# A graph attention layer: more edges get their keys and values by one-hot matmuls, and ScalarE writes a bias

## The chip, the cores and the metric

The kernel runs on one core of a Trainium2 chip. A core has TensorE (PE; matmuls, which write PSUM), VectorE (DVE), ScalarE (ACT), GpSimd (POOL) and SyncE (SP); each takes its instructions in order, and they wait for one another by semaphores. PEld is TensorE's weight load, which lies beside its matmuls. DMAs are issued from SP's and ACT's queues with addresses known to the queue, or from POOL's, which here reads 128 row numbers from SBUF and gathers those rows ("indirect DMA"). The metric is the device time of one execution in microseconds.

## What is computed

A graph has 6250 nodes with 64 features and 206250 edges sorted by destination. The reference, cut to what matters:

```python
Qh = (x @ Wq.T + bq).reshape(n, H, D)          # n = 6250, H = 4 heads, D = 16
Kh = (x @ Wk.T + bk).reshape(n, H, D)
Vh = (x @ Wv.T + bv).reshape(n, H, D)
Ee = (edge_attr @ We.T + be).reshape(-1, H, D)
score = (Kh[src] * Qh[dst] * (1.0 / np.sqrt(D)) * Ee).sum(-1)
score = jnp.exp(jnp.clip(score, -5.0, 5.0))
msg = Vh[src] * score[..., None]
wV = jax.ops.segment_sum(msg, dst, num_segments=n)
x = _layernorm(x + wV.reshape(n, H * D), axis=-1)
```

## The kernel before

**Tiles and steps.** 128 edges are a tile (1612 of them), 8 tiles a group. A step is two groups (16 tiles), the last eight steps one group each: 105 steps (`STEPS`, `NS`). The loop over steps starts at L708. In it the program text gives every engine its order by hand (`manual_schedule`); there is no planner.

**Before the loop.** k and v of all nodes are made and written to a table in DRAM (`kv_tab`, L315 to L324), then q in three bf16 parts (L340 to L361). The first four groups get k and v from gathered rows of x instead of the table (L230, L368 to L384): two transposes, an ACT copy, a bias matmul, two f32 matmuls and an ACT copy for each half group. Steps 2 and 3 are gathered (L402) before the branch at L412, whose other side handles unsorted inputs and does not run here.

**A step.** For step s: `products` (L602, L603: k times q times edge value, DVE), `scores` (L609 to L612: sum over a head, clip, exponent on ACT), `message` (L619 on DVE, L622 on ACT: v times score, and its first bf16 part), `minus` twice (L630, L632: the second and third bf16 part by a matmul with minus the identity), and in the next step `sums` (L638: 16 matmuls with the one-hot of destinations) and `add` (L652). For step s+1 it makes the one-hot rows (`spread` L555 on TensorE, L572 and L577 on ACT), the edge values (`edges`, L388 for the bias and L391), and the queries (L595). `small` (a PSUM tile) holds scores, sums and the row numbers that picking needs.

**k and v of a step** lie in one of five buffers `kvs`. They come in three ways. (1) Gathers on POOL: `gather(s+4)` stands behind `message(s)`, and its buffer is set free by that very product, so POOL starts when L619 is through. (2) Picking, for steps 4 to 94 (`picks_in`, L67), fills the last two tiles of step s+2: `sources` (L466, ACT) and `sources_turned` (L471, TensorE) spread the source numbers along the partitions; `hots` (L481, DVE, four for a step: two tiles, two halves) compares them with 25 block numbers at a time; `picks` (L491) multiplies 50 one-hot blocks with the table `parts` (x in three bf16 parts, 128 rows by 50 blocks), 25 matmuls a call; `picked` (L498, DVE) adds the three parts; `picked_turned` and `picked_kv` (L505 to L516) make k and v with f32 matmuls. Each picked tile is one gather less. (3) In every sixth step one column is fetched row by row from SP's queue (`fetch_rows`, L528 to L544; 16 or 24 rows in a step), which is one gather less in that step.

**The table `parts`** is set to zero (L427) behind the branch and made in steps 0 to 3 from seven loads of x (L448), with three ACT copies (L450, L451, L457) and two DVE subtractions (L456, L458) for each load.

The order of a step in the code, as the change finds it, starts with `onehot_rows` of the first next group and `sums(s-1)`, then `sources_turned`, `products(s)`, `edges(s+1, 0)`, `picks(s, 0, 0)`, `scores`, `onehot_rows_rest` of the second group, `message`, `gather`, `edges(s+1, 1)`, `minus`, `picks(s, 0, 1)`, `minus`, `picked_kv(s-1)`, `picks(s, 1, 0)`, `queries(s+1)`, `picks(s, 1, 1)`, and the hots of the next step. Sources for step s+1 and s+2 are prepared a step ahead.

## Time and profile before

| what | us |
|---|---|
| median of 10 runs (3072.1 to 3083.85) | 3078.01 |
| the profiled execution | 3074.86 |
| its span, first to last instruction | 3072.8 |
| busy: PE, PEld, DVE, ACT, POOL | 1982, 1554, 1504, 918, 1341 |
| mean granted TensorE clock (share of full) | 0.785 |
| gathers on POOL (L402), 1383 | 1308.5 |
| pick matmuls (L491), 9100 | 1040.7 |
| one-hots for picking (L481), 364 | 651.5 |

"Busy" is the time in which an engine has an instruction under way; matmuls overlap, so a matmul's mean duration is longer than the distance between two. "Idle before" a group is the time for which the engine stood still ahead of it, with what ended the wait; "issue" there means that the profile shows nothing it waited for, and "remote" that the releaser could not be named. In a timeline the columns are start, busy time, engine, line, operation, output<-inputs, shape and count, and in brackets the idle time before. In a table by stretches of time a row has the stretch, its length, busy time and number of instructions for PE, PEld, DVE, ACT and POOL, then the granted clock, the DMA share and GB/s.

### The profile page before, as it was taken

How to read it: one execution, taken by the hardware profiler on the slowest of the kernel's cores; microseconds unless marked ns; L12 is line 12 of the kernel's file. 1: busy time of each engine (PE TensorE's matmuls, PEld its weight loads, DVE VectorE, ACT ScalarE, POOL GpSimd, SP SyncE). 2: the span in 40 equal slices, each digit the busy share in tenths (PEclk: the TensorE clock that was granted, in tenths of full speed). 3: DMA queues.
4: the chain of work that ended last, by engine and by line, in shares of the span. 5: the costliest groups of instructions: out<-in, count | busy, mean ns of one | idle time of the engine just before them, and what ended most of it. 6: DMA issues, size and time to landing. Idle time of an engine off the chain costs nothing. (4 is left out here: it accounts for less than half of the span.)

```text
span 3072.8 us, 44286 instructions
## 1 busy us (share of the span) xinstructions
PE 1982.3 (65%) x15751; PEld 1554.2 (51%) x15751; DVE 1503.8 (49%) x1695; ACT 918.3 (30%) x1328; POOL 1340.6 (44%) x1427
## 2 busy tenths in 40 slices
PE   4546666657666666657566666757576666667665
PEld 4334555545454554545454554545454555545553
DVE  3234545545454545545454544545454554445554
ACT  2242332323232323323232232323232232223334
POOL 5455435344444434343444435343444434353342
PEclk9967878778787877778787877777787877777885
DMA  5222112111111111111111111111211111111111
GB/s 149 66 77 60 54 45 58 49 51 51 48 46 53 55 44 54 53 58 44 56 53 46 55 43 58 43 56 43 60 48 54 48 51 56 43 58 42 51 57 32
DMA packets 109970, 166.71 MB, mean 54 GB/s; under 512 B 69196, under 2 KB 71452, under 8 KB 109626
## 3 DMA queue, kind: packets, MB, share of 16 engines
q0 software_dynamic: 45280, 91.78, 10.4%
q1 hardware_dynamic: 64074, 71.01, 7.8%
q8 instruction: 125, 2.05, 0.3%
q10 hardware_dynamic: 384, 1.00, 0.2%
q14 instruction: 107, 0.88, 0.1%
HBM read 156.33 MB, written 7.33 MB: 53 GB/s over the span
## 5 line engine op out<-in xcount | busy, mean ns | idle before, releaser
L402 POOL DMA_INDIRECT kv<-kv_tab,src_i x1383 | 1308.5, 946 | 1677.0 <-DVE pq L619 1237.6
L491 PE MATMUL pick<-parts,hot 128*128 128x192 bf16 x9100 | 1040.7, 275 | 251.3 <-issue 250.6
L491 PEld LDWEIGHTS <-hot 128*128 128x128 bf16 x9100 | 890.3, 109 | 380.4 <-issue 323.3
L481 DVE TENSOR_TENSOR hot<-small,block 128x3200 bf16<-128x3200 bf16 x364 | 651.5, 1818 | 274.8 <-remote 247.9
L595 PE MATMUL pq<-qw,to 126*128 126x64 bf16 x1612 | 167.1, 220 | 679.7 <-issue 583.7
L572 ACT ACTIVATE to<-pb,minus_row 126x1024 bf16<-126x1024 f32 x202 | 223.0, 1104 | 1012.3 <-PE pb L555 958.1
L602 DVE TENSOR_TENSOR prod<-kv,pq 128x1024 f32<-128x1024 f32 (+2 forms) x105 | 123.7, 1178 | 799.4 <-PE pq L595 408.8
L595 PEld LDWEIGHTS <-to 126*128 126x128 bf16 x1612 | 109.3, 112 | 753.0 <-issue 750.3
L632 ACT ACTIVATE msg<-pq 128x1024 bf16<-128x1024 f32 (+2 forms) x210 | 207.8, 990 | 743.4 <-remote 480.2
L391 PE MATMUL pe<-we_sb,et 128*128 128x128 f32 x1612 | 247.9, 300 | 0.0
L391 PEld LDWEIGHTS pe<-we_sb,et 128*128 128x128 f32 x1612 | 207.9, 202 | 55.5 <-issue 50.6
L577 ACT ACTIVATE to<-to,one_p 126x1024 bf16<-126x1024 bf16 x202 | 230.4, 1141 | 3.5
L609 DVE TENSOR_REDUCE small<-prod 128x64 f32<-128x1024 f32 (+2 forms) x105 | 124.4, 1185 | 191.7 <-PE small L471 147.2
L638 PEld LDWEIGHTS <-of 128*128 128x128 bf16 x1612 | 156.6, 108 | 48.6 <-issue 37.7
L638 PE MATMUL small<-msg,of 128*128 128x192 bf16 x1612 | 171.6, 265 | 0.5 <-ACT msg L632 0.5
L630 PE MATMUL pq<-msg,minus_b 128*128 128x512 bf16 x404 | 126.9, 393 | 61.2 <-ACT msg L622 47.6
L555 PE MATMUL pb<-key_rows,ident_b 112*128 112x512 bf16 x403 | 151.4, 464 | 5.9 <-issue 4.7
L622 ACT ACTIVATE msg<-pq 128x1024 bf16<-128x1024 f32 (+2 forms) x105 | 103.9, 990 | 96.0 <-DVE pq L619 96.0
L603 DVE TENSOR_TENSOR prod<-prod,pe 128x1024 f32<-128x1024 f32 (+2 forms) x105 | 123.6, 1177 | 3.6
L619 DVE TENSOR_TENSOR pq<-kv,small 128x1024 f32<-128x1024 f32 (+2 forms) x105 | 123.5, 1176 | 1.4 <-ACT small L612 1.4
L585 DVE TENSOR_TENSOR of<-small,key 128x2048 bf16<-128x2048 bf16 (+2 forms) x105 | 123.2, 1173 | 0.3
L498 DVE TENSOR_REDUCE xp<-pick 128x128 f32<-128x384 f32 x91 | 50.8, 558 | 101.5 <-PE pick L491 101.5
(129 smaller groups left out, 991.3 us busy)
## 6 DMA issues: line engine op xcount, KB each, us to landing
et<-in_eT SPq DMA_DIRECT2D x100, 512.0 KB
rk<-kv_tab SPq DMA_DIRECT2D x1920, 0.5 KB
kv<-kv_tab,src_i POOLq DMA_INDIRECT x1383
qw<-q_tab SPq DMA_DIRECT2D x202, 15.8 KB
kv_tab<-kv_sb SPq DMA_DIRECT2D x5, 640.0 KB
q_tab<-q SPq DMA_DIRECT2D x5, 480.0 KB
acc<-in_x SPq DMA_DIRECT2D x48, 32.0 KB
out<-y SPq DMA_DIRECT2D x48, 32.0 KB
```

Source lines behind the costliest of these rows:

```text
L391: nc.tensor.matmul(pe[:, 2 * u:2 * u + 2, :], et[:, u, :], we_sb, start=False, stop=u == n // 2 - 1, skip_group_check=True)
L402: nc.gpsimd.indirect_dma_start(out=kv_of(g)[:, j, :], out_offset=None, in_=kv_tab[:, :], in_offset=bass.IndirectOffsetOnAxis(ap=src_i[:, t ...
L481: nc.vector.tensor_tensor(HOT[s, i, h].rearrange("p b (a c) -> p b a c", c=2), pairs(from_b[i])[:, None].to_broadcast(shape), block2[:, bl ...
L491: nc.tensor.matmul(rows3[:, i], hot[:, k, :], parts[:, b], start=b == 0, stop=b == NB - 1)
L555: nc.tensor.matmul(pb[:, b:b + 4, :], ident_b[:NR2, g // 2:g // 2 + 1].to_broadcast([NR2, P]), key_rows[:, g % 2, b * P:(b + 4) * P], star ...
L572: nc.scalar.activation(TO[g][:, :n, :], pb[:3 * W, :n, :], AF.Square, bias=minus_row3[:3 * W])
L577: nc.scalar.activation(TO[g][:, :n, :], TO[g][:, :n, :], AF.Relu, bias=one_p[:3 * W], scale=-1.0)
L595: nc.tensor.matmul(PQ[s][:, (g - STEPS[s][0]) * G + j, :], TO[g][:, j, :], QW[g], start=j == 0, stop=j == tiles_of(g) - 1, skip_group_chec ...
L609: nc.vector.tensor_reduce(score, prod[:, :n, :].rearrange("p g (h d) -> p g h d", h=H), axis=AX.X, op=OP.add)
L630: nc.tensor.matmul(msg[:, lo:hi, :], minus_b, M3[s][:, lo:hi, i, :], start=False, stop=True, skip_group_check=True)
L632: nc.scalar.activation(M3[s][:, :n, i + 1, :], msg[:, :n, :], AF.Copy)
L638: nc.tensor.matmul(PA[s], OH[s][:, j, :], M3[s][:, j], start=j == 0, stop=j == n - 1)
```

## The change

Picking starts at step 0 and ends two steps later (steps 0 to 96). In steps 0, 4, 8, ... 92 a third tile of step s+2 is picked, in the PSUM room of the second one: its half picks stand ahead of the queries, `picked_third` adds them up, and both halves of the second tile follow the queries. Step 2 and 3's picked tiles are not gathered before the branch. The table `parts` is made before the branch from the transposed x that is there anyway: 13 blocks of up to four transposes, two ACT copies and two DVE subtractions each, between the halves of the first k and v, which now turn the next half's x ahead of the current half. From step 1 on the edge values' bias is written into their PSUM tile by an ACT copy of a broadcast (`biases`), behind the exponent, and the bias matmul L388 is left out in the loop. `edges(s+1, 0)` moves behind `picked_turned`, `onehot_rows_rest` of the second group behind both edges. The column fetched row by row is the one before (index 12), as 13 can be picked now. The one-hots have six buffers instead of four, `far` three. Three buffers of the branch that does not run are made smaller.

```diff
 XG = 4
-TB = 8
-M0 = 4
+THIRD = 4
...
-LAST = NS - 8 - 3
+LAST = NS - 8 - 1
 def picks_in(s):
-    return M0 <= s <= LAST
+    return 0 <= s <= LAST
+def picks_third(s):
+    return picks_in(s) and s % THIRD == 0 and STEPS[s + 2][1] == 2
+def is_picked(g, j):
+    s = max(s for s in range(NS) if STEPS[s][0] <= g)
+    return picks_in(s - 2) and g == groups_of(s)[-1] and j >= (G - 3 if picks_third(s - 2) else G - 2)
...
-COLUMN = 2 * G - 3
+COLUMN = 2 * G - 4
...
+    parts = consts.tile([P, NB, 3, C], BF16, name="parts")
+    be_all = consts.tile([P, C], F32, name="be_all")
...
+        nc.sync.dma_start(be_all, beT.to_broadcast([P, C]))
...
+        halves = []
+        def parts_of_x(b):
+            n = min(TB, NB - b)
+            px = npsum.tile([P, 2, 2 * C], F32, name="ps").rearrange("p i (j c) -> p (i j) c", j=2)
+            px = px[:, :n]
+            for u in range(n):
+                nc.tensor.transpose(px[:, u, :], xT_sb[:C, (b + u) * P:(b + u + 1) * P],
+                                    ident[:C, :C])
+            nc.scalar.activation(parts[:, b:b + n, 0], px, AF.Copy)
+            nc.vector.tensor_sub(px, px, parts[:, b:b + n, 0])
+            halves.append((px, b, n))
+        def rest_of_x():
+            px, b, n = halves.pop(0)
+            nc.scalar.activation(parts[:, b:b + n, 1], px, AF.Copy)
+            nc.vector.tensor_sub(parts[:, b:b + n, 2], px, parts[:, b:b + n, 1])
+        order = [(g, h) for g in range(XG) for h in range(2)]
+        blocks = list(range(0, NB, TB))
+        xe = x_turned(*order[0])
+        for i, gh in enumerate(order):
+            following = x_turned(*order[i + 1]) if i + 1 < len(order) else None
+            for b in blocks[2 * i:2 * i + 2]:
+                parts_of_x(b)
+            first_kv(*gh, xe)
+            xe = following
+            while halves:
+                rest_of_x()
+    def edge_values(pe, et, n, biased=False):
+        if not biased:
+            nc.tensor.matmul(pe[:, :n, :], ones_b, be_p[:, :n, :], start=True, stop=False,
+                             skip_group_check=True)
...
     for g in range(XG, 2 * KVB - 2):
         for j in range(G):
-            gather_kv(g, j)
+            if not is_picked(g, j):
+                gather_kv(g, j)
...
-            parts = accp.tile([P, NB, 3, C], BF16, name="parts")
-            nc.vector.memset(parts, 0.0)
-            NX = N // NB
...
+            pe_all = fixed.tile([P, 2 * G, C], F32, name="pe")
...
-            def table_parts(b):
-                n = min(TB, NB - b)
-                raw = work.tile([P, TB, C], F32, name="raw", bufs=1)
-                nc.sync.dma_start(raw[:NX, :n], x_v[:, b:b + n, :])
-                rest = pick[:NX, :n * C].rearrange("p (b c) -> p b c", b=n)
-                nc.scalar.activation(rest, raw[:NX, :n], AF.Copy)
-                nc.scalar.activation(parts[:NX, b:b + n, 0], raw[:NX, :n], AF.Copy)
...
+            def wanted(s, i):
+                return picks_third(s) if i == 2 else picks_in(s)
...
-                if picks_in(s):
-                    FAR[s, i] = work.tile([P, P], BF16, name="far")
-                    nc.scalar.activation(FAR[s, i], row50, AF.Identity,
-                                         bias=src_f[:, s - M0, i:i + 1], scale=-1.0)
+                if wanted(s, i):
+                    FAR[s, i] = work.tile([P, P], BF16, name="far", bufs=3)
+                    nc.scalar.activation(FAR[s, i], row50, AF.Identity, scale=-1.0,
+                                         bias=src_f3[:, thirds.index(s):][:, :1] if i == 2 else
+                                         src_f[:, s, i:i + 1])
...
-                if picks_in(s):
-                    HOT[s, i, h] = work.tile([P, NB // 2, P], BF16, name="hot", bufs=4)
+                if wanted(s, i):
+                    HOT[s, i, h] = work.tile([P, NB // 2, P], BF16, name="hot", bufs=6)
...
-                if picks_in(s):
+                if wanted(s, i):
                     hot = HOT.pop((s, i, h))
                     for k in range(NB // 2):
                         b = h * NB // 2 + k
-                        nc.tensor.matmul(rows3[:, i], hot[:, k, :], parts[:, b], start=b == 0,
-                                         stop=b == NB - 1)
+                        nc.tensor.matmul(rows3[:, min(i, 1)], hot[:, k, :], parts[:, b],
+                                         start=b == 0, stop=b == NB - 1)
+            def picked_third(s):
+                if picks_third(s):
+                    X[s] = work.tile([P, 3, C], F32, name="xp")
+                    nc.vector.tensor_reduce(X[s][:, 0], rows3[:, 1].rearrange("p i c -> p c i"),
+                                            axis=AX.X, op=OP.add)
...
                 if picks_in(s):
                     room = psum.tile([P, G, P], F32, name="pb")
-                    nc.tensor.transpose(room[:, 0, :], X[s].rearrange("p k c -> p (k c)"), ident)
-                    xe = work.tile([P, P], F32, name="xe")
-                    nc.scalar.activation(xe, room[:, 0, :], AF.Copy)
-                    X[s] = xe, room[:, 4:6, :]
+                    xe = work.tile([P, 2, P], F32, name="xe")
+                    nc.tensor.transpose(room[:, 0, :], X[s][:, 1:].rearrange("p k c -> p (k c)"), ident)
+                    if picks_third(s):
+                        nc.tensor.transpose(room[:C, 1, :], X[s][:, 0], ident)
+                    nc.scalar.activation(xe[:, 0], room[:, 0, :], AF.Copy)
+                    if picks_third(s):
+                        nc.scalar.activation(xe[:C, 1], room[:C, 1, :], AF.Copy)
+                    X[s] = xe, room[:, 4:7, :]
             def picked_kv(s):
                 if picks_in(s):
                     xe, kv = X.pop(s)
-                    nc.tensor.matmul(kv, ones_b, bkv_p[:, :2], start=True, stop=False,
+                    lo = 0 if picks_third(s) else 1
+                    n = tiles_in(s + 2)
+                    nc.tensor.matmul(kv[:, lo:], ones_b, bkv_p[:, lo:3], start=True, stop=False,
                                      skip_group_check=True)
-                    nc.tensor.matmul(kv, xe, wkv, start=False, stop=True, skip_group_check=True)
-                    nc.scalar.activation(kvs[(s + 2) % KVB][:, 2 * G - 2:, :], kv, AF.Copy)
+                    nc.tensor.matmul(kv[:, 1:], xe[:, 0], wkv, start=False, stop=lo == 1,
+                                     skip_group_check=True)
+                    if lo == 0:
+                        nc.tensor.matmul(kv[:, 0], xe[:C, 1], wkv[:C, 0], start=False, stop=True,
+                                         skip_group_check=True)
+                    nc.scalar.activation(kvs[(s + 2) % KVB][:, n - 3 + lo:n, :], kv[:, lo:], AF.Copy)
...
-                        if not picks_in(s - 2) or g == STEPS[s][0] or j < G - 2:
+                        if not is_picked(g, j):
                             gather_kv(g, j)
...
             def edges(s, k):
                 g = STEPS[s][0] + k
-                if k == 0:
-                    PE[s] = psum.tile([P, 2 * G, C], F32, name="pe")
-                edge_values(PE[s][:, k * G:(k + 1) * G], ET[g], tiles_of(g))
+                PE[s] = pe_all
+                edge_values(PE[s][:, k * G:(k + 1) * G], ET[g], tiles_of(g), s > 0)
+            def biases(s):
+                n = tiles_in(s)
+                nc.scalar.activation(pe_all[:, :n, :], be_all[:, None, :].to_broadcast([P, n, C]),
+                                     AF.Copy)
...
             closed, scaled, normed = 0, 0, 0
+            for i in (0, 2):
+                sources(0, i)
+                sources_turned(0, i)
...
+            sources(0, 1)
+            sources(1, 0)
+            for i, h in ((0, 0), (0, 1), (2, 0)):
+                hots(0, i, h)
...
                     sums(s - 1)
                 sources_turned(s, 1)
                 sources_turned(s + 1, 0)
+                sources_turned(s + 1, 2)
...
-                making = [b for b in range(s * 2 * TB, (s + 1) * 2 * TB, TB) if b < NB]
-                if making:
-                    rest = table_parts(making[0])
                 prod = products(s)
                 picked(s - 1)
-                if more:
-                    edges(s + 1, 0)
                 picks(s, 0, 0)
                 score = scores(s, prod)
-                if nexts[1:]:
-                    onehot_rows_rest(nexts[1])
+                if more:
+                    biases(s + 1)
                 if s:
                     add(s - 1)
                 msg = message(s, score)
                 if s + KVB - 1 < NS:
                     gather(s + KVB - 1)
                 picked_turned(s - 1)
+                if more:
+                    edges(s + 1, 0)
                 if nexts[1:]:
                     edges(s + 1, 1)
+                    onehot_rows_rest(nexts[1])
                 minus(s, msg, 0)
                 hots(s, 1, 0)
+                hots(s, 2, 1)
                 picks(s, 0, 1)
+                picks(s, 2, 0)
                 minus(s, msg, 1)
+                picks(s, 2, 1)
                 picked_kv(s - 1)
                 if not more:
                     close(B - 2)
                     spreads(B - 2)
                 hots(s, 1, 1)
-                picks(s, 1, 0)
+                if not picks_third(s):
+                    picks(s, 1, 0)
                 sources(s + 1, 1)
                 sources(s + 2, 0)
+                sources(s + 2, 2)
                 if s + 1 < NS:
                     rows_fetched(s + 1)
                 if more:
...
                         keys(nexts[0] * G)
                     onehot_edges(s + 1)
                     queries(s + 1)
-                picks(s, 1, 1)
+                if not picks_third(s):
+                    picks(s, 1, 1)
                 hots(s + 1, 0, 0)
+                picked_third(s)
+                if picks_third(s):
+                    picks(s, 1, 0)
+                    picks(s, 1, 1)
                 hots(s + 1, 0, 1)
+                hots(s + 1, 2, 0)
                 if more:
                     while closed < B - 2 and due[closed] <= s:
...
                         if normed < scaled:
                             norm(normed)
                             normed += 1
-                for i, b in enumerate(making):
-                    if i:
-                        rest = table_parts(b)
-                    table_parts_rest(b, rest)
             assert normed == B - 2
```

Line numbers of before are those of the profile.

## The prediction

> **What bounds the kernel now.** I read the page first, then the times at which the message product (DVE, L619) starts, which cut the run into steps, then TensorE inside one step, then clock and gathers beside it.
>
> The page (share of the span; then groups: busy, mean ns | idle before, releaser):
>
> ```profile
> span 3072.8 us, 44286 instructions
> PE 1982.3 (65%) x15751; PEld 1554.2 (51%) x15751; DVE 1503.8 (49%) x1695; ACT 918.3 (30%) x1328; POOL 1340.6 (44%) x1427
> ...
> L402 POOL DMA_INDIRECT kv<-kv_tab,src_i x1383 | 1308.5, 946 | 1677.0 <-DVE pq L619 1237.6
> L491 PE MATMUL pick<-parts,hot 128*128 128x192 bf16 x9100 | 1040.7, 275 | 251.3 <-issue 250.6
> ...
> L595 PE MATMUL pq<-qw,to 126*128 126x64 bf16 x1612 | 167.1, 220 | 679.7 <-issue 583.7
> ```
>
> No engine is full. The gathers wait for the messages, not the reverse, and TensorE stands idle 680 us before its query matmuls, 584 of it for nothing that the profile shows. TensorE in step 39 (message at 1301.87), in order of time:
>
> ```profile
> 1304.41 0.59 PE L630 MATMUL pq<-msg,minus_b 128*128 128x512 bf16 x2
> 1304.84 2.23 PE L491 MATMUL pick<-parts,hot 128*128 128x192 bf16 x25
> ...
> 1308.17 1.79 PE L491 MATMUL pick<-parts,hot 128*128 128x192 bf16 x18
> ...
> 1314.42 0.37 PE L595 MATMUL pq<-qw,to 126*128 126x64 bf16 x4 [2.16 <-issue]
> ...
> 1323.11 0.53 PE L595 MATMUL pq<-qw,to 126*128 126x64 bf16 x7 [1.18 <-issue]
> 1323.45 4.19 PE L491 MATMUL pick<-parts,hot 128*128 128x192 bf16 x25
> 1327.43 0.74 PE L555 MATMUL pb<-key_rows,ident_b 112*128 112x512 bf16 x2
> 1328.01 1.49 PE L638 MATMUL small<-msg,of 128*128 128x192 bf16 x16
> ```
>
> Up to 1309.5 it runs without a gap, then it starts some 17 matmuls in 13.6 us, 0.7 or 1.4 us apart, and at 1323.1 it runs freely again. The 14 gathers of the step (POOL) start from 1303.35 to 1319.61. I call the time from 1309.5 to 1323.1 the slow stretch. It ends 2.6 us after the last gather in every step that I looked at, so it belongs to the gathers. The 25 picks behind it take 4.19 us, those ahead of it 2.23, as the granted clock says (sixth figure after the stretch's length):
>
> ```profile
> 1302.00:1314.00 12.00, 8.88 (x80) 6.91 (x79) 8.10 (x6) 3.11 (x5) 8.21 (x9) 1.00 0.16 45
> 1314.00:1327.60 13.60, 5.93 (x42) 4.93 (x42) 4.01 (x4) 1.33 (x4) 5.03 (x6) 0.50 0.25 73
> ```
>
> So a step is: gathers, slow stretch (over 21.3 us after the message), then what TensorE has left, picks first, then sums and the score that ends in the next message: 9.3 us. Message products of selected steps:
>
> ```profile
> 204.70 1.22 DVE L619 TENSOR_TENSOR pq<-kv,small 128x1024 f32<-128x1024 f32 x1
> 228.13 1.22 DVE L619 TENSOR_TENSOR pq<-kv,small 128x1024 f32<-128x1024 f32 x1
> ...
> 2294.78 1.22 DVE L619 TENSOR_TENSOR pq<-kv,small 128x1024 f32<-128x1024 f32 x1
> 2325.43 1.22 DVE L619 TENSOR_TENSOR pq<-kv,small 128x1024 f32<-128x1024 f32 x1
> 2353.05 1.22 DVE L619 TENSOR_TENSOR pq<-kv,small 128x1024 f32<-128x1024 f32 x1
> ...
> 2964.51 1.22 DVE L619 TENSOR_TENSOR pq<-kv,small 128x1024 f32<-128x1024 f32 x1
> 2979.93 1.22 DVE L619 TENSOR_TENSOR pq<-kv,small 128x1024 f32<-128x1024 f32 x1
> ```
>
> Step 72: 30.65 us with picks and 14 gathers. Step 73: 27.62 with picks and 13 gathers. Step 2: 23.43 with no picks and 14 gathers. Step 95: 15.42 with no picks and 8 gathers, where step 92 (message at 2895.40, next 2919.27) takes 23.87 with picks and 8. A pick is not free: its matmuls sit where TensorE is on the path, and a gather taken away gives back less.
>
> The sum is made against the profiled execution, 3074.86 us (2.06 around its span). The median of the runs is 3.15 above it.
>
> **The change part by part.**
>
> *Picks in steps 0 to 3.* The old intervals from message 0 (153.46) to message 4 (251.77) sum to 98.3. With picks they become like step 4 (picks, 14 gathers, no row fetches yet on SP): 251.77 to 281.26, 29.5. One of the four is a third-pick step (29.5 + 4, below), one has 13 gathers (27.7), two have 14: 120. **+22**, ends +14 (all 28) and +34 (all like step 72). The loads and copies of the old table (7 loads on SP, 21 ACT copies of 0.55, 14 DVE subtractions of 0.64) leave these steps; they lay in the slow stretch, where DVE waited 7 to 11 us, so I count nothing for them.
>
> *Before the loop.* Steps 2 and 3 gather 27 tiles, not 32. Gathers start 1.25 apart (72.38, 73.63), and the making of q crawls until 109, behind the last of them: -6. The first k and v (L375 to L384) run 3.03 us per half, eight halves, TensorE without a gap (114.92 to 139.5). The change puts 50 transposes of 64 rows in between. Nearest row is L350 (64 columns, f32): 12 in 2.79, so 0.23 each, +11.5 (ends 0, and 16 by L375's 0.32). The 26 ACT copies (0.38 by L378) and 26 DVE subtractions lie beside it. Ahead of message 0 the 4.06 us memset of the table goes and three hots of 1.82 come; DVE waited 1.23 there, so about +1. One more load of the edge bias on SP is early and hidden. **+6.5**, ends 0 and +13.
>
> *The third pick.* 24 steps (0, 4, ... 92); 22 of them between step 4 and 91. Each adds 50 picks on TensorE, two hots (3.6 us) and one reduce on DVE, one ACT copy of 0.39 and one of 0.27, one transpose and one or two small matmuls. DVE's and ACT's share is covered: DVE waits 8.16 us ahead of L602 in step 39, ACT 9.73 ahead of L572. Where that cover went, 4.2 us of DVE would come on the path. TensorE has no such cover. Ahead of the slow stretch it is busy without a gap, in the stretch it gets through its 17 whatever they are, so 50 more go behind it. The order puts the queries ahead of both halves of pick 1, so the products start no later, but sums(s) still follow the last pick. Price: behind the stretch the first 25 or so run at 0.16, as before; by then 4.6 us have passed and the clock is 1.00 (1327.6 on), so 50 at 0.083 (2.23 for 25, less the overlap) are 4.1, and 0.1 for the small ones. 4.2 x 22 = **+92**. Ends: 2.1 each if half of them are covered (+46); 8.3 if all run at half clock (+183). I take the full clock, since the rows at 1327.43 on show it. In pick 1 a wait is added: its first matmul needs the DVE reduce of the third pick. Queued behind it are 50 picks and the sums. The three key and value matmuls and 16 queries stand between (some 1.5 us), which hides a 0.56 reduce.
>
> The Trainium skill, page "TensorE: Matmul & The Clock Gate", section "What's actually happening", says that about 3.4 us of sustained work give the full clock. By that rule the stretch at half clock would be 1.2 us shorter than the 4.6 seen, and the added picks still run warm: the same 92.
>
> *Fewer gathers.* 22 intervals lose one gather. Step 76 (14 gathers, 16 row fetches on SP, 2414.32 to 2444.22) takes 29.90, step 73 with as many row fetches and 13 gathers 27.62: -2.3 here, about -2.1 over all such steps; the end of the slow stretch itself moves by 1.45 (21.3 to 19.85). Step 73 has its TensorE order unchanged, the new steps carry more, so I take -1.8: **-40**, ends -28 (1.25, a gather's own spacing) and -62 (2.8, step 72 to 73).
>
> The same skill, page "SBUF — State Buffer", section "Who interferes with whom", says that DMA never contends with a compute engine. By it a gather less would shorten nothing and this term would be 0; the trace (13.6 us of crawl beside 14 gathers, less beside 13) speaks against it.
>
> *The bias.* Two matmuls of L388 go per step (0.31 between starts, 0.62 in all), and an ACT copy of 128x1024 comes (1.02 by L622). It stands where L577 (1.14) stood, between the exponent and the first message copy, and L577 moves behind the latter; there ACT idled 0.88 before L622 and 7.3 before the second L632. So ACT pays nothing; if it came on the path, the first L632 starts 0.4 later, +20 with half the steps. TensorE's 0.62 lies ahead of L630, which starts at 1304.41, while L622 ends at 1304.15: only 0.15 to 0.2 can be won. What is late next is that ACT copy. 92 x -0.15 = **-14**, ends -57 and +20. The edge values of the first group move behind the first picks and are needed a step later: nothing.
>
> *The end.* Steps 95 and 96 get picks: 15.42 to 23.9 (step 92), 14.41 to about 22.4. Step 94 gets its last 25: 21.31 to 23.9. Step 92 is a third (+4), and 92 and 93 each lose two gathers of 1.22. Sum **+18**, ends +10 and +24. The steps behind are half as large and their gathers start as before.
>
> Sum: 22 + 6.5 + 92 - 40 - 14 + 18 = +84.5, so 3159 on the profiled execution and some 3162 on the median; I say 3160.
>
> **The rivals.**
> A (forecast): the third pick lies bare behind the slow stretch. 3160; its own range 3115 to 3215.
> B (faster): the extra picks go where TensorE idles, because the stretch limits something other than the number of matmuls. For it: 584 us of idle with no releaser. Against it: steps 5 to 92 alike get through 6 to 23 matmuls there, picks or queries. Third pick 0 gives 84.5 - 92 = -7.5, 3067; with the bias at its end 3024. It decides where a third pick costs under 0.36 us.
> C: TensorE stays at half clock through all picks: 4.1 more, 22 times: 3250. For it: the slow stretch is when the clock falls. Against: 1.00 is granted 4.6 us after it.
> D: ACT's new copy delays the message chain by 0.4 to 1 us: 37 to 92 more, 3197 to 3252. Against: the 0.88 of idle.
>
> **How the numbers follow.** A 0.62, B 0.10, C 0.12, D 0.12; 0.04 for no change within 0.2%, which is about what a measurement of this kernel can tell. All low ends together give 3026, all high 3321; leaving 2 in 10 out gives 3076 to 3250. Faster 0.10, same 0.04, slower 0.86.
>
> **What would show it.** Right: intervals of steps 4, 8, 12 near 34 to 35 us with 75 to 85 matmuls behind the slow stretch before L638, its end unmoved; intervals 5, 9, 13 near 28.5; the others within 0.5 of before; steps 0 to 3 near 30. The bias right: L630 0.1 to 0.2 sooner after the message. Wrong: if the third-pick steps are as long as their neighbours, the picks found cover; if all steps shorten by half a microsecond or more, the bias was on the path; if steps 0 to 3 stay near 24, picks are cheaper than they look.

## The result and the profile after

The changed kernel takes 3158.36 us in the median of 8 runs (3155.53 to 3167.25), the kernel before 3078.24 in 28 runs beside it: ratio 1.0266, 95% interval 1.0257 to 1.0275. The change makes the kernel slower, by 80 us, where 82 were forecast (3160 against 3078). The profiled execution of after took 3165.68 us, 7.3 above its median; that of before lies 3.2 below its own. So the traces differ by 90.8 us, and the shares below are shares of that.

The page of after: engines, then the groups that answer to those shown of before (gathers, picks, queries).

```profile
span 3163.9 us, 48270 instructions
PE 2107.1 (67%) x17533; PEld 1685.1 (53%) x17533; DVE 1631.1 (52%) x1811; ACT 1013.0 (32%) x1509; POOL 1303.0 (41%) x1391
...
L449 POOL DMA_INDIRECT kv<-kv_tab,src_i x1347 | 1271.0, 944 | 1802.0 <-DVE pq L681 1363.7
L531 PE MATMUL pick<-parts,hot 128*128 128x192 bf16 x10900 | 1227.0, 270 | 382.4 <-issue 379.5
...
L657 PE MATMUL pq<-qw,to 126*128 126x64 bf16 x1612 | 155.3, 223 | 514.5 <-issue 433.2
```

36 gathers fewer free 37.5 us of POOL, which waits for messages anyway (its idle time ahead of the gathers went from 1677 to 1802). 1800 picks more are 186 us of TensorE's busy time. Its idle time ahead of the queries shrank by 165 us and that ahead of the picks grew by 131: in the steps with a third pick, the slow stretch is now filled with picks, where queries stood in it.

Message products of a step with a third pick (40), of the one behind it with 13 gathers (41), and the first steps:

```profile
157.70 1.23 DVE L681 TENSOR_TENSOR pq<-kv,small 128x1024 f32<-128x1024 f32 x1 [0.28 <-ACT small L674]
191.55 1.22 DVE L681 TENSOR_TENSOR pq<-kv,small 128x1024 f32<-128x1024 f32 x1
219.60 1.22 DVE L681 TENSOR_TENSOR pq<-kv,small 128x1024 f32<-128x1024 f32 x1
...
1384.49 1.22 DVE L681 TENSOR_TENSOR pq<-kv,small 128x1024 f32<-128x1024 f32 x1
1418.05 1.22 DVE L681 TENSOR_TENSOR pq<-kv,small 128x1024 f32<-128x1024 f32 x1
1446.61 1.22 DVE L681 TENSOR_TENSOR pq<-kv,small 128x1024 f32<-128x1024 f32 x1
```

The gathers that run after message s are those for step s+5, since message s frees the buffer of that step (there are five); in the program text they stand behind message s+1. So step 41 has 13 gathers because of the third pick of step 44, which fills a tile of step 46.

Step 40 takes 33.56 us, step 41 28.56. Over the 22 steps of each kind between 4 and 91, the mean interval went from 30.30 to 34.22 where a third pick is made, from 29.92 to 28.43 in the step behind it, from 30.40 to 30.39 and from 29.55 to 29.69 in the other two. Interval 0 (with a third pick) is 33.85, interval 1 28.05; they were 26.71 and 24.53.

TensorE in step 40, in order of time (start, length, and in brackets the idle time before):

```profile
1387.24 4.29 PE L531 MATMUL pick<-parts,hot 128*128 128x192 bf16 x50
1391.37 0.59 PE L692 MATMUL pq<-msg,minus_b 128*128 128x512 bf16 x2
...
1396.70 0.41 PE L531 MATMUL pick<-parts,hot 128*128 128x192 bf16 x3 [1.69 <-issue]
1398.10 0.32 PE L531 MATMUL pick<-parts,hot 128*128 128x192 bf16 x1 [0.99 <-issue]
...
1407.02 1.01 PE L657 MATMUL pq<-qw,to 126*128 126x64 bf16 x16
1407.84 5.64 PE L531 MATMUL pick<-parts,hot 128*128 128x192 bf16 x50
1413.31 0.60 PE L612 MATMUL pb<-key_rows,ident_b 112*128 112x512 bf16 x2
1413.75 1.49 PE L700 MATMUL small<-msg,of 128*128 128x192 bf16 x16
```

The picture is that of before with 50 picks more in it. TensorE runs freely to 1392, crawls until about 1406.3, which is 21.8 us after the message (21.3 before), and then has all 50 picks of the second tile in front of the sums, where before it had 25. (I call the slow stretch the crawl as well.) The table of stretches of step 40 (as before: matmuls in brackets, granted clock in the sixth figure after the length):

```profile
1384.49:1396.50 12.01, 8.84 (x84) 7.54 (x85) 9.27 (x7) 3.36 (x5) 8.09 (x9) 1.00 0.15 44
1396.50:1406.30 9.80, 3.43 (x14) 1.56 (x14) 0.12 (x1) 0.36 (x1) 5.13 (x6) 0.52 0.15 43
1406.30:1418.00 11.70, 11.58 (x117) 10.18 (x115) 8.02 (x13) 5.61 (x9) 0.00 (x0) 0.81 0.19 52
```

117 matmuls stand behind the crawl up to the next message, TensorE is busy for 11.58 of the 11.70 us, and POOL has nothing to do there.

Step 40 is one of the mildest. In the mean of the 20 steps with a third pick from 12 to 91, the crawl (taken up to the last idle time of TensorE over 0.3 us ahead of the sums) ends 21.55 us after the message, where it ended at 21.30 in the same steps of before. From there to the sums TensorE does 76 matmuls (68 to 85) in 8.32 us, where it did 30 in 4.69; what follows the sums is as long as before (4.30 against 4.34). So the whole 3.9 us lies between the crawl and the sums.

### The profile page after: what moved, and what is told of

It reads as the page before. It is cut to its first block, busy times and chain, and to the rows that moved or that the text cites. A ratio compares the mean times of both kernels' runs of the same rounds, so it can differ in the third digit from the quotient of the medians.

```text
span 3163.9 us, 48270 instructions
## 1 busy us (share of the span) xinstructions
PE 2107.1 (67%) x17533; PEld 1685.1 (53%) x17533; DVE 1631.1 (52%) x1811; ACT 1013.0 (32%) x1509; POOL 1303.0 (41%) x1391
## 5 line engine op out<-in xcount | busy, mean ns | idle before, releaser
L449 POOL DMA_INDIRECT kv<-kv_tab,src_i x1347 | 1271.0, 944 | 1802.0 <-DVE pq L681 1363.7
L531 PE MATMUL pick<-parts,hot 128*128 128x192 bf16 x10900 | 1227.0, 270 | 382.4 <-issue 379.5
L531 PEld LDWEIGHTS <-hot 128*128 128x128 bf16 x10900 | 1032.5, 107 | 562.5 <-issue 481.6
L521 DVE TENSOR_TENSOR hot<-small,block 128x3200 bf16<-128x3200 bf16 x436 | 773.4, 1816 | 0.0
L657 PE MATMUL pq<-qw,to 126*128 126x64 bf16 x1612 | 155.3, 223 | 514.5 <-issue 433.2
L438 PE MATMUL pe<-we_sb,et 128*128 128x128 f32 x1612 | 215.0, 287 | 48.7 <-ACT pe L626 46.4
L438 PEld LDWEIGHTS pe<-we_sb,et 128*128 128x128 f32 x1612 | 194.0, 196 | 73.9 <-ACT pe L626 70.4
L538 DVE TENSOR_REDUCE xp<-pick 128x64 f32<-128x192 f32 x24 | 8.6, 358 | 305.9 <-PE pick L531 232.5
L612 PE MATMUL pb<-key_rows,ident_b 112*128 112x512 bf16 x403 | 140.2, 433 | 1.0 <-ACT to L634 1.0
```

What stands on the lines that cost most here:

```text
L438: nc.tensor.matmul(pe[:, 2 * u:2 * u + 2, :], et[:, u, :], we_sb, start=False, stop=u == n // 2 - 1, skip_group_check=True)
L449: nc.gpsimd.indirect_dma_start(out=kv_of(g)[:, j, :], out_offset=None, in_=kv_tab[:, :], in_offset=bass.IndirectOffsetOnAxis(ap=src_i[:, t ...
L521: nc.vector.tensor_tensor(HOT[s, i, h].rearrange("p b (a c) -> p b a c", c=2), pairs(from_b[i])[:, None].to_broadcast(shape), block2[:, bl ...
L531: nc.tensor.matmul(rows3[:, min(i, 1)], hot[:, k, :], parts[:, b], start=b == 0, stop=b == NB - 1)
L612: nc.tensor.matmul(pb[:, b:b + 4, :], ident_b[:NR2, g // 2:g // 2 + 1].to_broadcast([NR2, P]), key_rows[:, g % 2, b * P:(b + 4) * P], star ...
L657: nc.tensor.matmul(PQ[s][:, (g - STEPS[s][0]) * G + j, :], TO[g][:, j, :], QW[g], start=j == 0, stop=j == tiles_of(g) - 1, skip_group_chec ...
```

## The experiments

Each kernel was compared with the kernel before on the same chip, and four chips were used. Before took 3073.99 us on the chip of a1_no_third, a2_bias_matmul, a3_third_no_matmuls and b1_no_picks, 3095.02 on that of b2_no_picks_no_rows, b3_half_gathers, c1_early_pick and c2_late_pick, 3081.36 on that of b4_no_rows, c3_pick_last and c5_pick_last_no_rows, and 1790.08 on that of c6_late_pick_no_rows, which is a finding of its own, told there. Totals are compared across chips only as ratios to before.

**Undoing parts of the change.** Three kernels start from after.

*a1_no_third* makes no third pick; everything else of the change stays.

```diff
 def picks_third(s):
-    return picks_in(s) and s % THIRD == 0 and STEPS[s + 2][1] == 2
+    return False
```

> The changed kernel without the third pick: the tile is gathered again, all else is as changed. Theory T (matmuls behind the slow stretch lie bare): the third-pick intervals fall from 34.2 to 30.3 us (24 times, -93) and the intervals that had one gather less get 1.45 us longer (23 times, +34), net -59 from 3158: 3100. Rival M (the cost lies in the moved order, the bias copy or the early and late picks): it stays above 3140.

Measured: 3094.47 us, ratio 1.0075 (1.0057 to 1.0092). The four kinds of steps have means of 30.26, 29.59, 30.27 and 29.58, as before the change (30.30, 29.92, 30.40, 29.55). The third pick is 1.9 of the 2.7 per cent; the picks of steps 0 to 3 and the rest are 0.75.

*a2_bias_matmul* gives the bias of the edge values back to TensorE.

```diff
-                edge_values(PE[s][:, k * G:(k + 1) * G], ET[g], tiles_of(g), s > 0)
+                edge_values(PE[s][:, k * G:(k + 1) * G], ET[g], tiles_of(g))
...
-                if more:
-                    biases(s + 1)
```

> The changed kernel with the bias matmul back in place of the ScalarE copy, order as changed. Theory T by the two traces, in which the intervals of plain steps stayed at 30.4 us: 3153 to 3163. Rival W (the copy wins 0.15 us a step, as the prediction had it): 3172. Rival X (the copy is itself in the way, TensorE waited 46 us for it in the changed kernel): 3110 to 3145.

Measured: 3156.86 us, ratio 1.0282 (1.0261 to 1.0303), against 1.0266 (1.0257 to 1.0275) with the copy on ScalarE: no difference that can be told. The run changes both at once, so it shows that the exchange is worth nothing, not what each side is. The traces add where the gain went: with the copy, the first matmul of `minus` starts 2.33 us after the message in the median step (2.54 in before, 2.55 to 2.66 in a2_bias_matmul), so TensorE is 0.2 us sooner there, and the steps without a third pick are no shorter for it (30.39 and 29.69 against 30.32 and 29.63).

*a3_third_no_matmuls* keeps the third pick's one-hots, reduce, transposition and copies, and the gather it saves, but does 2 of its 50 matmuls, so the third tile's k and v are not computed.

```diff
                     for k in range(NB // 2):
+                        if i == 2 and k != h * (NB // 2 - 1):
+                            continue
                         b = h * NB // 2 + k
```

> The changed kernel with 2 of the 50 matmuls of each third pick, so that the third tile's keys and values are wrong; its one-hots, its reduce, its copies and its gather left out are as changed. Theory T (TensorE pays): the third-pick intervals fall by 3.9 us and the shorter gathers stay, 3158 - 93 = 3065. Rival V (DVE's two one-hots and the wait on the reduce pay): above 3140.

Measured: 3073.32 us, ratio 0.9999 (0.9989 to 1.0009). Steps with a third pick fall from 34.22 to 30.65, the steps behind stay at 28.25. So 48 matmuls are 3.57 us of a step, 0.074 each, and the two one-hots of 1.8, the reduce, the copies and the 2 matmuls left are together no more than about 0.4 (30.65 against 30.26 in a1_no_third, on the same chip). In this kernel the gathers saved make up for all the rest of the change.

**What picks cost at all.** *b1_no_picks* is the kernel before with no pick: all 16 tiles of a step gathered.

```diff
 def picks_in(s):
-    return M0 <= s <= LAST
+    return False
...
-            nc.vector.memset(parts, 0.0)
...
-                making = [b for b in range(s * 2 * TB, (s + 1) * 2 * TB, TB) if b < NB]
+                making = []
```

> The kernel before with no picks at all: 16 gathers in every step (15 where a column is fetched row by row), no one-hots, no table. Theory T: the slow stretch ends 1.49 + 16 x 1.22 + 2.4 = 23.4 us after the message and 2.6 us of work follow as in step 3 of before, so 26 us instead of 30.0 in steps 4 to 91: about 2700. Rival P (a pick earns its place: two gathers more cost 2.1 to 2.8 us each): 3300 or more.

Measured: 2745.78 us, ratio 0.8921 (0.8899 to 0.8944). It is faster than both kernels. Without picks the intervals from 4 to 91 have a mean of 26.59 us, with two picks and two gathers fewer 30.04. What follows the last gather is short here: from its start to the next message product 6.4 us in the mean of steps 12 to 89, against 12.5 in the kernel before and 13.5 in after. The sums start 8.2 us after the message here, ahead of the last gather's end in every step from 12 to 89; in before they start at 25.7 and in after at 26.4, behind it in every step. TensorE has nothing left by then (step with messages at 1294.13 and 1319.43, one with 15 gathers; granted clock in the sixth figure after the length):

```profile
1302.00:1312.00 10.00, 7.08 (x38) 4.89 (x36) 2.44 (x2) 2.26 (x2) 7.56 (x9) 0.80 0.24 60
1312.00:1319.43 7.43, 0.00 (x0) 0.10 (x1) 2.12 (x4) 2.01 (x3) 1.76 (x2) 0.55 0.10 27
```

*b3_half_gathers* leaves half of the gathers of steps 12 to 96 out; k and v of those tiles are not fetched.

```diff
                     for j in range(tiles_of(g)):
+                        if 12 <= s < 97 and j % 2:
+                            continue
```

> The kernel before, with every second gather of steps 12 to 96 left out (7 or 8 remain per step; the k and v of those tiles are stale, so this leaves out half of the fetching of k and v). Theory T (the slow stretch belongs to the gathers): seven gathers started 1.25 us apart from 1.49 us after the message end at 9.9, so the stretch ends near 12.5 us after the message instead of 21.3. About 8 matmuls fewer get through in the stretch and are done behind it (about +1 us), so an interval is about 30.4 - 8.75 + 1 = 22 to 23 us, 85 intervals, total 2400 to 2450. Rival U (TensorE starts its matmuls late for a reason of its own, the gathers only lie beside it): intervals stay above 29, total 3000 or more.

Measured: 2344.24 us, ratio 0.7571 (0.7559 to 0.7584); the mean interval is 21.4 from step 8 on, a little below T's 22 to 23, and the total is below its 2400 to 2450. One step (message at 1050.45, next 1072.81), TensorE in order of time:

```profile
1056.76 1.40 PE L491 MATMUL pick<-parts,hot 128*128 128x192 bf16 x15
1058.34 0.24 PE L491 MATMUL pick<-parts,hot 128*128 128x192 bf16 x1 [0.17 <-issue]
...
1061.89 0.48 PE L491 MATMUL pick<-parts,hot 128*128 128x192 bf16 x2 [1.00 <-issue]
1063.06 1.01 PE L597 MATMUL pq<-qw,to 126*128 126x64 bf16 x16 [0.69 <-ACT msg L634]
1063.88 4.19 PE L491 MATMUL pick<-parts,hot 128*128 128x192 bf16 x25
```

The seven gathers start from 1051.94 to 1059.43; the crawl ends at 1063.06, 12.6 us after the message, where T gave 12.5. What stands behind it is as long as before (9.8 us against 9.3). So the crawl lasts as long as the gathers, and what TensorE has left behind it is added bare. Whether it is the gathers' DMA traffic or something else about them that holds TensorE, this run does not separate.

**Where a pick stands.** Three kernels make one pick per step instead of two, so 15 gathers, and differ in the place of its 50 matmuls. *c1_early_pick* keeps the one that starts ahead of the second message copies:

```diff
-                        if not picks_in(s - 2) or g == STEPS[s][0] or j < G - 2:
+                        if not picks_in(s - 2) or g == STEPS[s][0] or j != G - 2:
...
             def picks(s, i, h):
+                if i != 0:
+                    return
```

(the same return in the functions for the sources and one-hots; the reduce and the last copy take one tile).

> The kernel before with one picked tile per step instead of two: the one whose 50 matmuls stand ahead of the slow stretch; the other tile is gathered again, so a step has 15 gathers. Without picks an interval was 26.6 us (16 gathers, 25.3 with 15), with both it is 30.04. Theory P (place: TensorE is idle ahead of the stretch in the kernel without picks, so a pick that is worked off there is free and one gather less is won): intervals 25.2 to 26, total 2620 to 2700. Rival S (count: some 60 matmuls run freely behind a message and some 15 in the stretch, whichever they are; 50 more, wherever they stand, push 35 to 40 behind the stretch and the sums with them): intervals about 28, total 2850 to 2930.

Measured: 3050.63 us, ratio 0.9871 (0.9848 to 0.9893), mean interval 29.69. Both theories fail: one pick, and by P the cheap one, costs nearly as much as two. The trace shows where the time goes: in ACT, which copies the message for TensorE (messages at 1301.98 and 1333.54; TensorE first, then ACT):

```profile
1306.82 0.59 PE L639 MATMUL pq<-msg,minus_b 128*128 128x512 bf16 x2
1307.26 2.45 PE L499 MATMUL pick<-parts,hot 128*128 128x192 bf16 x25
1318.97 1.01 PE L639 MATMUL pq<-msg,minus_b 128*128 128x512 bf16 x2 [9.27 <-ACT msg L641]
...
1326.20 1.01 PE L604 MATMUL pq<-qw,to 126*128 126x64 bf16 x16 [4.74 <-ACT msg L641]
```

```profile
1317.90 1.02 ACT L641 ACTIVATE msg<-pq 128x1024 bf16<-128x1024 f32 x1 [11.09 <-remote]
1325.12 1.02 ACT L641 ACTIVATE msg<-pq 128x1024 bf16<-128x1024 f32 x1 [6.20 <-remote]
```

The two matmuls that the first of these copies needs are on record at 1306.82, and the copy starts 11 us later. In the trace's semaphore events TensorE's counter stands still meanwhile: it rises at 1306.51, 1314.33, 1317.87 and 1325.10, and the copies follow the last two. So in the crawl not only TensorE's starts are late; what it has on record as done (the second of these matmuls at 1307.42) is reported late to the engines that wait for it. Whether the report is late or the record early, the trace does not tell. Here the last copy is pushed behind the gathers and queries, spreads, sums and edge values behind it: 8.4 us to the next message.

*c2_late_pick* keeps the other tile (the condition has `j != G - 1`, the return `i != 1`) and moves both halves behind the queries:

```diff
-                picks(s, 1, 0)
...
                     queries(s + 1)
+                picks(s, 1, 0)
                 picks(s, 1, 1)
```

> The mirror of c1_early_pick: one picked tile per step, the one whose matmuls come late, with both its halves put behind the queries of the next step; 15 gathers. Theory P (place): all 50 lie bare behind the slow stretch, 25 at half and 25 at full clock (6.3 us), so the interval is about 22.5 + 6.3 + 3 = 31 to 32 us and the total 3050 or more, at least 350 above c1_early_pick. Rival S (count): the same number of matmuls is left behind the stretch as in c1_early_pick, interval about 28, total within 60 us of c1_early_pick.

Measured: 3081.76 us, ratio 0.9956 (0.9939 to 0.9972), mean interval 30.15, 31 us above c1_early_pick. Again neither: the total lies in P's range, the difference in S's. The second message copy starts 5 us after the message (20 in c1_early_pick; both are means), the queries at 5.7 in the step looked at; the picks then fill the crawl, and spread, sums and edge values, which stand behind them in the order, come after it.

*c3_pick_last* moves the 50 matmuls behind the spreads and sums too, a step later, and what follows from them behind the message. *c5_pick_last_no_rows* is the same without the row fetches on SP.

```diff
                     onehot_rows(nexts[1], spread(nexts[1]))
+                if s:
+                    picks(s - 1, 1, 0)
+                    picks(s - 1, 1, 1)
...
-                picks(s, 1, 0)
-                picks(s, 1, 1)
```

```diff
 def is_rowed(s):
-    return s % ROWED == 0 and 2 * ROWED <= s < NS - 8
+    return False
```

> One picked tile per step as in c2_late_pick, but with its 50 matmuls put behind everything of TensorE that leads to the next message: behind the second spread and the sums of the step, one step later in the program (and the reduce, the transposition and the k and v of the picked tile behind the message). Theory O (order: TensorE gets to the end of what is ordered ahead of the slow stretch, and a pick costs what it pushes from there to behind the stretch; c1_early_pick pushed the second message copy, 20 us after the message instead of 5.5, c2_late_pick the sums and spreads): the message copies, queries and sums are through before the stretch as in the kernel without picks, so the interval is 25.3 to 27 us, total 2620 to 2800. Rival N (50 more matmuls of TensorE, or 1.8 us of one-hot twice on DVE, cost 3 us in any place): interval 29 or more, total 2950 to 3100.

> c3_pick_last without the tile of every eighth step whose rows are fetched one by one on SP. Without picks, leaving these out made the kernel faster (2717 against 2762 for the same chip's scale). Theory O: 0 to 40 us below c3_pick_last, so 2600 to 2780, about the kernel without picks and rows or below it. Rival N: 2920 or more.

(The expectations speak of every eighth step; the row fetches serve every sixth.) Measured: c3_pick_last 3017.16 us, ratio 0.9799 (0.9782 to 0.9815), as N said; c5_pick_last_no_rows 2703.83 us, ratio 0.8759 (0.8727 to 0.8790), as O said, with most intervals at 25.2. Neither theory expected a difference of 313 us between them. The traces take O's side as to the mechanism. In c5_pick_last_no_rows the sums start ahead of the last gather's end in 59 of the 78 steps from 12 to 89, and these steps take 25.26 us; in the other 19 they start behind it, and these take 28.38. In c3_pick_last 75 of the 78 are of the second kind, with 29.42. TensorE around the message at 1341.74, in a step of 25.22 us whose last gather ends at 1361.66:

```profile
1348.15 0.63 PE L604 MATMUL pq<-qw,to 126*128 126x64 bf16 x16 [1.00 <-ACT msg L641]
...
1357.02 1.01 PE L564 MATMUL pb<-key_rows,ident_b 112*128 112x512 bf16 x2 [7.40 <-issue]
1357.82 2.77 PE L647 MATMUL small<-msg,of 128*128 128x192 bf16 x16
```

And around the message at 1287.65, in a step of 28.87 us whose last gather ends at 1307.55:

```profile
1285.48 4.68 PE L499 MATMUL pick<-parts,hot 128*128 128x192 bf16 x50
...
1292.81 0.59 PE L639 MATMUL pq<-msg,minus_b 128*128 128x512 bf16 x2
1294.52 0.59 PE L639 MATMUL pq<-msg,minus_b 128*128 128x512 bf16 x2 [1.11 <-issue]
...
1310.67 1.01 PE L564 MATMUL pb<-key_rows,ident_b 112*128 112x512 bf16 x2 [12.19 <-ACT kv L525]
```

The picks run across the message, where the gathers have only begun. The spread, and the sums behind it, wait for ACT's copy of the picked tile's k and v (last line, L525). This copy starts 15.7 us after the message in the median step of c5_pick_last_no_rows and 22.9 in c3_pick_last, with the last gather's end at 19.9 and 19.7 in the mean. So N is out, and O's place is not enough by itself: with row fetches the same order leaves the sums behind the gathers. The other kernels fit: in b1_no_picks and b2_no_picks_no_rows all sums come ahead of the last gather's end (26.46 and 26.10 us a step), in before, after, c2_late_pick and b4_no_rows all come behind it (29.5 to 30.7), and in c1_early_pick 67 of 78 come behind it (30.04, the other 11 take 27.81).

**The row fetches.** They are 128 single fetches on SP for one tile of every sixth step, in both kernels, and they are spread over the steps, 16 or 24 in each. (Where the expectations count 11 steps, it is 15.)

*b2_no_picks_no_rows* takes them out of b1_no_picks, *b4_no_rows* out of the kernel before, with the edit shown above.

> The kernel without picks, and without the tile of every eighth step whose rows are fetched one by one on SP: 16 gathers in every step. Theory T (the interval follows the number of gathers, SP's single fetches cost nothing else): 11 intervals gain 1.4 us, total 15 above the kernel without picks, about 2761. Rival R (SP's row fetches slow all steps as they compete with the gathers): total 2720 or less.

> The kernel before without the tile of every eighth step whose rows are fetched one by one on SP: its other picks and gathers stay. Theory G (a step's time follows its gathers and what stands behind the slow stretch): 11 steps gain a gather, worth 2.3 us each by steps 72 and 73, so +25 us, ratio 1.008. Rival R (the 128 fetches and their instructions cost more than the gather they save, as they did in the kernel without picks): ratio 0.985 to 0.995.

Measured: b2_no_picks_no_rows 2717.27 us, ratio 0.8775 (0.8761 to 0.8790), against 0.8921 with them; b4_no_rows 3022.45 us, ratio 0.9808 (0.9791 to 0.9824). The rivals hold, and more: leaving them out is worth 1.9% in the kernel before, although its steps gain gathers. A tile fetched row by row is dearer than a gather.

**The last run.** *c6_late_pick_no_rows* is c2_late_pick without row fetches, to tell whether the place of the picks or the row fetches made c5's time.

> c2_late_pick without the tile of every eighth step whose rows are fetched one by one on SP. It differs from c5_pick_last_no_rows (2704, against 3081 of before) only in the place of the 50 matmuls: behind the queries, ahead of the second spread and the sums. Theory O (the place decides: the sums are pushed behind the slow stretch): what the rows give is about what they gave in the kernel before (ratio 0.981), so c2_late_pick's 0.9956 becomes about 0.975, 3000 to 3030. Rival R (the row fetches alone held c3_pick_last back, and the place is nothing): within 2% of c5_pick_last_no_rows, ratio 0.87 to 0.895.

Measured: 1922.27 us (1922.17 to 1922.33); before on the same chip 1790.08 (1789.73 to 1790.50); ratio 1.0739 (1.0721 to 1.0757). Neither theory is tested, because there is no slow stretch on this chip. The same kernel before takes some 1284 to 1305 us less here than on the three others. Idle times of TensorE over 0.3 us with nothing shown that it waits for come 8.8 times a step in the trace of before, and not once in this one (steps 12 to 89). The groups, TensorE in one step, and ACT and POOL beside it (messages at 897.68 and 916.53):

```profile
PE 1477.6 (77%) x11110; PEld 1104.7 (58%) x11110; DVE 1175.0 (61%) x1604; ACT 883.2 (46%) x1222; POOL 1437.4 (75%) x1533
...
L402 POOL DMA_INDIRECT kv<-kv_tab,src_i x1489 | 1405.3, 944 | 453.8 <-issue 434.0
```

```profile
900.00 0.59 PE L639 MATMUL pq<-msg,minus_b 128*128 128x512 bf16 x2 [2.17 <-ACT msg L631]
901.71 1.01 PE L639 MATMUL pq<-msg,minus_b 128*128 128x512 bf16 x2 [1.11 <-ACT msg L641]
...
904.86 5.94 PE L499 MATMUL pick<-parts,hot 128*128 128x192 bf16 x50
```

```profile
900.63 1.02 ACT L641 ACTIVATE msg<-pq 128x1024 bf16<-128x1024 f32 x1 [0.51 <-PE pq L639]
```

```profile
903.42 0.95 POOL L402 DMA_INDIRECT kv<-kv_tab,src_i  x1 [0.30 <-issue]
904.68 0.94 POOL L402 DMA_INDIRECT kv<-kv_tab,src_i  x1 [0.31 <-issue]
```

Gathers take the 0.94 us they took, 1.25 apart, but they no longer wait for messages, and TensorE does 50 picks in 5.94 us beside them. The copy starts 0.6 us after its matmuls, not 11. The chain that ended last is POOL's gathers for 55% of the span, and the mean interval 18.29 is close to 15 gathers of 1.25. So here a step seems to cost what its gathers cost: this kernel has 106 gathers more than before (1489 against 1383) and takes 132 us longer, 1.25 for each. By that the 36 gathers that the change saves would be worth about 45 us there. That is an estimate from this pair, in which row fetches and picks differ too; the changed kernel was not run on this chip, and whether it is faster there is open.

## Why the prediction was right, and where its terms were off

The mechanism forecast is the one found: the third pick's matmuls lie bare between the end of the slow stretch and the sums (a1_no_third, a3_third_no_matmuls, and the counts of the 20 steps above). That 80 us came where 82 were forecast is in part luck: the bias term was 17 us too low and the end 14 us too high, and the two nearly cancel. The steps of the sum, in the traces (their difference is 90.8 us, the forecast sum 84.5):

| term | forecast (ends) | measured |
|---|---|---|
| before the loop | +6.5 (0, 13) | +4.2: message 0 from 153.5 to 157.7 |
| steps 0 to 3 get picks | +22 (14, 34) | +22.7: 98.3 to 121.0 |
| third pick, 22 steps | +92 (46, 183) | +86.3: 22 x 3.92 |
| one gather fewer, 22 steps | -40 (-28, -62) | -32.8: 22 x -1.49 |
| bias copy | -14 (-57, +20) | +2.9 in the other 44 steps; a2_bias_matmul: no difference |
| the end, steps 92 to 96 | +18 (10, 24) | +4.0 |
| behind it, steps 97 to 103 | 0 | +3.5 |

The likeliest case A was the right one, and each rival has a run against it. B (the picks go into TensorE's idle time) would have left steps with a third pick as long as their neighbours; they are 3.9 us longer, and a3_third_no_matmuls shows that it is the matmuls. C (half clock throughout) is out by the sum: 34.22, not 38. D (ACT's copy delays the message) is out: the first matmul of `minus` starts 0.2 us sooner after the message with the copy, not 0.4 to 1 later, and a2_bias_matmul, without it, is no faster.

Three terms were off, the bias, the end and the gather; the third pick came out by its working. *The bias* was mis-sized: it took TensorE's time ahead of the second message copies as time on the path. The 0.2 us were won there, as forecast (2.33 us after the message against 2.54), and the steps were no shorter: the crawl stands behind that place, and its end belongs to the gathers. The same reason that priced the third pick should have priced this at nothing. So the sign that the prediction named for this term, `minus` 0.1 to 0.2 sooner, came, and says nothing about the time.

*The end* was mis-sized: its intervals were 25.4, 21.5, 23.9, 23.9 and 22.4, measured 22.2, 18.6, 21.2, 22.3 and 18.7. The "+4" of a third pick does not hold for step 92, which had 8 gathers: it got shorter by 1.7 us, and with two gathers fewer at 1.22 that leaves 0.8 for the pick, by estimate. I had taken the price from steps with 14 gathers. Why steps 93 to 96 also came out shorter than forecast, no run shows.

*The third pick's* price of 4.2 came out at 3.92, and by the working given. In the mean of 20 steps 46 matmuls more stand between the crawl's end and the sums (76 against 30, where 75 to 85 in all were forecast), and they take 3.63 us more, 0.079 each, near the 0.083 taken for the full clock; the crawl itself ends 0.25 later. That not all of the 50 stand there is what keeps the price a little under 4.2.

*A gather less* gave 1.49 us where 1.8 was taken: the 1.45 by which the crawl's end moves was the better row, not the 2.3 read from steps 73 and 76. Between a1_no_third, where these steps have their gather back, and a3_third_no_matmuls, on the same chip, it is 1.34 (29.59 and 28.25).

One reading of the prediction was incomplete: in the slow stretch of step 39 the matmuls start 0.7, 1.4 or 2.1 us apart (1316.12, 1318.21, 1320.32), not 0.7 or 1.4 alone. No term rests on it.

The prediction set the page "SBUF — State Buffer" of the Trainium skill (section "Who interferes with whom"), which says that DMA never contends with a compute engine, against the trace. By that rule a gather fewer would have been worth 0; it was worth 1.49 us a step, and with half of the gathers the run took 0.757 of its time. The last run narrows this: on one chip the same gathers ran beside TensorE without holding it up. So the rule fits what was seen on that chip and not what was seen on the other three.

What stays open: why ACT's copy of the picked k and v comes so much later with the single-row fetches (22.9 us after the message against 15.7), which goes with 0.9799 of the time of before instead of 0.8759. The run that was to separate place and row fetches fell on the chip without a slow stretch. And what, on three chips of four, holds TensorE up while the gathers run: it is not the gathers' own duration, and not their number alone, since the fourth chip has both.

## What to carry to other kernels

Price a piece of work by what its engine has to do at the point where the last other wait ends: here 50 matmuls in place of one gather were dear, because TensorE's backlog stood bare behind the gathers. Look first whether the work that leads to the next step (here the sums) starts ahead of the other engine's end or behind it, in many steps and not in one: the traces divide by that. Before tuning such a trade, run the kernel once without the feature (b1_no_picks was 10.8% faster than the kernel before) and on a second chip: here another engine was the bound there.

## What the runs showed of the hardware

- On three chips TensorE, with matmuls to do, starts them 0.7, 1.4 or 2.1 us apart while indirect gathers run, from some 6 to 7.5 us after the first gather's start (one step each of before, after, b3_half_gathers and c2_late_pick), and this ends 2.6 us (with seven gathers 2.7) after the last gather's end. It is not so in every step: in c5_pick_last_no_rows, after 7.4 us of idle time, 18 matmuls run in 3.6 us (from 1357.02) while gathers run on to 1361.66. On the fourth chip there is none of it, with the same gathers of 0.94 us, 1.25 apart: 1790.08 us against 3074 to 3095 for the same kernel.
- During this crawl TensorE's semaphore rises late by the trace: a copy that needs matmuls on record at 1306.82 starts at 1317.90; on the fourth chip the same pair of instructions lies 0.6 us apart.
- Leaving out the single-row fetches on SP, and gathering that tile, takes the kernel before to 0.9808 of its time, and the kernel with one pick placed last from 3017 to 2704 us.
- The fastest kernels on the chips with a slow stretch that fetch all of k and v are c5_pick_last_no_rows (0.8759) and b2_no_picks_no_rows (0.8775), which can't be told apart by these ratios, each taken on its own chip.
